# GpSimd's queue in program order, another order of seven products in the first block of a pass, and another order of tile addresses

## The chip, the cores and the metric

The kernel runs on one core of a Trainium2 chip. The core has TensorE (PE, matrix products), VectorE (DVE), ScalarE (ACT), GpSimd (POOL) and SyncE (SP); each takes its own instructions in order, and they wait for one another on semaphores. Transfers are done by 16 DMA engines; SP, ACT and POOL issue them. The metric is device time in microseconds (us). Before the change the median of three runs is 2068.01 us (2066.77 to 2068.09).

## The reference

Attention without softmax, in which keys times values are summed up along the sequence, and a mixture of experts in which all experts share one pair of weights. Cut to what matters:

```python
xn = layernorm(x)                               # 4 sequences x 1024 tokens x 1024
q = xn @ Wq.T + bq;  k = xn @ Wk.T + bk;  v = xn @ Wv.T + bv
phi_q = elu(q) + 1;  phi_k = elu(k) + 1
kv_sum = cumsum(phi_k * v, axis=1)
s = (phi_q * kv_sum) * SCALE @ Wo.T + bo
# router: top 2 of 8 experts per token, at most 256 tokens (CAP) each, in order
buf[dest] = xn[token]
h = gelu(buf @ w1.T + b1) @ w2.T + b2           # w1: 4096 x 1024, w2: 1024 x 4096
gathered = where(keep, h[dest], 0) * prob
out = zeros.at[token_idx].add(gathered)
return x + s * silu(out)
```

An expert holds at most 256 tokens, and tokens beyond that get nothing, so only the first tokens can have a g that isn't zero. The kernel works out which tokens these are, and computes queries, the result product and the feed-forward products for them alone. Everything is float32; a product of two float32 matrices is made of three products of their high and low parts (fp32r).

## The kernel before

**Two phases.** In the first (0 to 452.8 us) the keys and values of all tokens are projected (lines 160 to 162), summed up along the sequence on VectorE, transposed into tiles `kr` and stored to `kvs` in memory; the router fills lists of tokens. In the second, 140 product steps run one after another on TensorE (`multiply`, matmul in line 1005). Each step is one of the seven products of a Strassen-like scheme for a 2 x 2 block product, and has 48 matmuls of 128 x 128 by 128 x 512.

**The order of steps.** There are NP = 2 passes of 70 steps. A pass has NQ = 4 times a `hidden` block (7 steps, w1, gelu) and an `ffn_out` block (7 steps, w2), then a `queries` block (7 steps, Wq) and a `result` block (7 steps, Wo). `hidden` and `queries` go through `features`, `ffn_out` and `result` through `outputs`. The first step of pass 1 (the second pass) is n = 71, of its queries n = 127, of its result n = 134; of pass 0 they are 1, 57 and 64.

**Operands.** The left operand `a` and the right `b` of step n are two `Unit` tiles each (u = 0, 1), taken from three places in turn. `cast` (ScalarE, line 793) writes the high half, `low` (VectorE, line 796) the low half. In `features` of pass 0's first block the right operand is made in the same way, from token tiles in `work`, and then stored to memory (`xtd<-b`, line 1100, on SP) for the blocks that follow, which load it (`b<-xtd`, line 976, on SP). For pass 1 the tokens are prepared beside steps 15 to 34 by `xprep_items`: gathers on GpSimd (line 647), transposes and subtractions on VectorE, then seven split tiles `o` for each of four token blocks, stored to `xtd` on GpSimd (line 679).

**Weights.** The quarters of a weight matrix lie in five tiles `raw`. They are loaded on SP (line 766 for w1 and Wq, line 1055 for w2 and Wo), and VectorE makes the sums that the seven products need (`sub`, line 930; `plus`, line 933). `left_weights` does this for `features`: it loads the quarters (0,0), (1,0), (1,1) and (0,1) at steps n0-4 to n0-1, and makes one difference in step n0 and a sum and a difference at the start of step n0+1.

**The order by hand.** `on(n, phase, f)` hangs work onto a phase of step n, and the phases run in the order load, pre, cast0, evac, low0, add, cast1, low1, post, raw (line 905). PE, DVE, ACT and SP keep the order in which the program issues their work. GpSimd's order is left to a scheduler, except where `in_turn` (lines 233 to 236) pins an instruction, and that only outside the hand-made order. The row loads (line 1182 for `b2`, line 1272 for `bo`), the stores of line 679 and the scatters that add into `out` (line 1292) are not pinned.

**Results.** The products are summed in two PSUM tiles of four banks. `chains` says which products share one PSUM tile: in `features` the order is ROWS = (1, 6, 2, 7, 5, 4, 3) with groups (1, 2), (6, 7, 4), (5, 3). The first result of a block is copied by ScalarE to a quarter of `hid` (line 1113), the others are added by VectorE (line 933). In `result` the last quarters lie in `hid`, `ht` and `y`; they are multiplied by the gate (line 1322) and scattered to `out` by GpSimd (line 1292, four scatters a quarter). The next `hidden` block writes to the same `hid`.

**Queries.** `fetch` gathers a quarter of `kvs` into two small tiles `gk`, `turn` transposes it to two small tiles `kv` on VectorE (line 240, four instructions of 128 x 512 a quarter), ScalarE makes the exponentials (lines 1222 and 1223), and `then` joins them (lines 1228 and 1233). The quarter (0,1) is fetched at step n0+1 and turned at step n0+3.

**Small tiles.** `small` takes tiles of 4 KB a partition from a pool `sp` with nine buffers in rotation (line 896). It holds what `xprep_items` gathers, turns and splits, the temporary `t`, the rows `b2` and `bo`, `gk`, `kv`, `ex`, and the parts of the result. A new tile waits for the last user of the old one in its buffer. The pool stands ahead of `fp`, which holds three of the `raw` tiles, `y0` and the third place of a and b.

Of the kernel before, what the change touches and what calls it, by code (L numbers as in the profile page):

```python
# [18 lines left out]
P = 128  # L19
# [27 lines left out]
def tile_first_tokens(  # L47
# [43 lines left out]

    xtd = [dp.tile([7 * 2 * P, 4 * BT], F32, name=f"xtd_{p}") for p in range(NP)]

# [139 lines left out]
    def in_turn(ins):  # L233

        if not in_order[0]:
            tc.keep_in_program_order(ins)

    def turned(dst, g):

        t = nc.vector.transpose(  # L240
            dst.rearrange("p c (b j) -> p b c j", j=SQ),
            g.rearrange("p (b c i) -> p b c i", b=NA, i=SQ),
        )
        in_turn(t)

# [409 lines left out]
    def xprep_items(p, buf):  # L655

        def item(j):
            g, v = {}, {}  # L660

            def fetch():
                for i in range(2):
                    g[i] = buf(f"g{p}_{j}_{i}")
                    slots[2 * p + i].quarters(g[i], xnd, j)

            def turn():
                for i in range(2):
                    r = buf(f"x{p}_{j}_{i}")
                    turned(r.rearrange("p (c t) -> p c t", c=DC), g[i])  # L670
                    v[0, i], v[1, i] = r[:, :BT], r[:, BT:]

            def out_of(i, src):
                o = buf(f"o{p}_{j}_{i}")
                oh = o.bitcast(F32R).rearrange("p (u h k t) -> h p u k t", u=2, h=2, k=2)
                split((oh[0], oh[1]), src.rearrange("p (u k t) -> p u k t", u=2, k=2))
                dst = xtd[p].rearrange("(i u p) (s t) -> i u p s t", i=7, u=2, s=4)[i - 1]
                for u, ou in enumerate(o.rearrange("p (u s t) -> u p s t", u=2, s=4)):
                    nc.gpsimd.dma_start(dst[u, :, :, j * P : (j + 1) * P], ou)  # L679

            def plain():
                out_of(1, v[0, 0])
                out_of(2, v[1, 0])

            def sums():
                t = buf(f"t{p}_{j}")
                v["t1"], v["t2"] = t[:, :BT], t[:, BT:]
                nc.vector.tensor_tensor(v["t1"], v[0, 1], v[0, 0], ALU.subtract)
                nc.vector.tensor_tensor(v["t2"], v[1, 1], v["t1"], ALU.subtract)
                out_of(6, v["t2"])  # L690

            def sums2():
                nc.vector.tensor_tensor(v[0, 1], v[1, 1], v[0, 1], ALU.subtract)
                nc.vector.tensor_tensor(v[1, 0], v[1, 0], v["t2"], ALU.subtract)
                out_of(7, v[0, 1])
                out_of(5, v["t1"])

            def rest():
                out_of(4, v[1, 0])
                out_of(3, v[1, 1])  # L700

            return fetch, turn, plain, sums, sums2, rest

        return [item(j) for j in range(NJ)]
# [74 lines left out]
    class Unit:  # L779


        def __init__(self, side, i):

            pool = later["fu" if (i + 1) % 3 < 2 else "fp"]
            self.t = pool.tile(
                [P, 2, 2 * BT], F32R, tag=f"{side}{(i + 1) % 3}", name=name(side)
            )

# [38 lines left out]
    with tc.manual_schedule(engines=order), tc.tile_pool(name="rp", bufs=1) as rp:  # L827
# [13 lines left out]
        for b in range(nhead):  # L841
# [17 lines left out]
            if b == nhead - 1:  # L859
# [17 lines left out]
                put([[sl.load] for sl in slots], at=28 // half)  # L877
                put([[lambda i=i: left_quarter(raw[i], w1, i, 0)] for i in range(2)])
            kv_block(parts, stream, list(turn[2:]) if b == 0 else [], b == nhead - 1)
# [15 lines left out]

    sp = ctx.enter_context(tc.tile_pool(name="sp", bufs=9, reuse_waits="tile"))

    sp.tile([P, 2 * P], F32, tag="room", bufs=1, name="room")
    fp = ctx.enter_context(tc.tile_pool(name="fp", bufs=1, reuse_waits="tile"))
    later["fp"] = fp  # L900
    fps = ctx.enter_context(tc.tile_pool(name="fps", bufs=2, space=PSUM, reuse_waits="tile"))
    bq1, nbq = (cp.tile([P, DC], F32, name=n) for n in ("bq1", "nbq"))
# [13 lines left out]

    raw += [quarter(f"raw_{i}") for i in range(2, 5)]
    hid = big.tile([P, 4, NK, BT], F32, tag="xt", name="hid")
# [4 lines left out]
    yq = {(i, j): work[:, 2 * i + j] for i in range(2) for j in range(2)}  # L923
    yq[0] = quarter("y0")

# [55 lines left out]
    def tokens(p, i):  # L981
        return xtd[p].rearrange("(i u p) f -> i u p f", i=7, u=2)[i - 1]

# [31 lines left out]

    ROWS = (1, 6, 2, 7, 5, 4, 3)
    COLS = (1, 2, 6, 5, 7, 3, 4)

# [6 lines left out]

    def left_weights(n0, src, view=None):

        q = dict(zip(((0, 0), (1, 0), (1, 1), "t", (0, 1)), raw))
        raw[:] = (q[k] for k in ((0, 0), "t", (1, 0), (1, 1), (0, 1)))

        def load(*keys):
            for key in keys:
                left_quarter(q[key], src, *key)

        if n0:
            on(n0 - 4, "raw", lambda: load((0, 0)))
            on(n0 - 3, "raw", lambda: load((1, 0)))
        on(max(n0 - 2, -1), "raw", lambda: load((1, 1)))
        on(n0 - 1, "raw", lambda: load((0, 1)))

        on(n0, "add", lambda: sub(q["t"], q[0, 0], q[1, 0]))
        on(n0 + 1, "pre", lambda: plus(q[1, 0], q[1, 0], q[1, 1]))
        on(n0 + 1, "pre", lambda: sub(q[0, 0], q[1, 0], q[0, 0]))
        on(n0 + 3, "add", lambda: sub(q[0, 1], q[0, 1], q[0, 0]))
        for k, key in enumerate(((0, 0), (0, 0), (0, 1), "t", (1, 0), (1, 1), (0, 1))):
            built(n0 + 1 + k, "a", lambda key=key: q[key], by_blocks, of_blocks)

# [35 lines left out]

    def right_tokens(n0, p):
        if n0:
            for k, i in enumerate(ROWS):
                fetched(n0 + 1 + k, p, i)
            return

        x = {(i, j): work[:, 2 * j + i] for i in range(2) for j in range(2)}  # L1090
        t2 = hq["t"]
        on(1, "add", lambda: sub(x[0, 0], x[1, 1], t2))
        on(3, "add", lambda: sub(x[1, 0], x[1, 0], t2))
        keys = {1: (0, 0), 2: (1, 0), 3: (1, 1), 4: (1, 0), 5: (0, 0), 7: (0, 1)}
        for k, i in enumerate(ROWS):
            built(1 + k, "b", lambda i=i: t2 if i == 6 else x[keys[i]], by_chunks, all_chunks)

            def keep(k=k, i=i):
                for u in range(2):
                    nc.sync.dma_start(tokens(p, i)[u], flat(plan_at(1 + k)["b"][u]))  # L1100

            on(k + 1, "raw", keep)

    def features(n0, p, src, act, then=None):

        h = dict(hq)
        left_weights(n0, src)
        right_tokens(n0, p)
        chains(n0, ROWS, ((1, 2), (6, 7, 4), (5, 3)))
        ps = {k: plan_at(n0 + k)["ps"] for k in range(1, 8)}  # L1110

        def e1():
            nc.scalar.copy(whole(h[1, 0]), whole(ps[1][0]))

# [10 lines left out]
        if then:  # L1125
            for k, key, src in (
# [5 lines left out]
                )  # L1132
        on(n0 + 2, "evac", e1)
        on(n0 + 3, "evac", lambda: more(2, (0, 1), (1, 0)))
        on(n0 + 4, "evac", c11)
        on(n0 + 5, "evac", lambda: more(4, (1, 1), (1, 0)))
        on(n0 + 6, "evac", lambda: last(5, (1, 1), (1, 1)))
# [7 lines left out]
    def hidden(n0, p, s):  # L1145
# [4 lines left out]

        return features(n0, p, w1[s * DC : (s + 1) * DC], act)

# [6 lines left out]
    def ffn_out(n0, h, s, y):  # L1159
# [18 lines left out]
        if s == 0:  # L1178

            def row():  # L1180
                y["b"] = small("b2")
                nc.gpsimd.dma_start(y["b"], rows[0:1, :].broadcast_to([P, D]))

            on(n0, "load", row)
# [6 lines left out]
    def queries(n0, p):  # L1191
# [48 lines left out]
        for k, d, key in (  # L1240
            (-14, 2, (0, 0)), (-12, 2, (1, 1)), (-6, 3, (1, 0)), (1, 2, (0, 1))
        ):
# [22 lines left out]
    def result(n0, h, y, p):  # L1265
# [4 lines left out]
        def row():  # L1270
            c["b"] = small("bo")
            nc.gpsimd.dma_start(c["b"], rows[1:2, :].broadcast_to([P, D]))

# [13 lines left out]
        def done(key, parts):  # L1287
            i, j = key
            for m in range(4):
                src = parts(m)  # L1290
                apart(
                    nc.gpsimd.indirect_dma_start(  # L1292
                        out=out.rearrange("n (a f) -> (n a) f", a=2),
                        out_offset=bass.IndirectOffsetOnAxis(
                            ap=slots[2 * p + i].half[:, j, m : m + 1], axis=0
                        ),
                        in_=src,
                        in_offset=None,
                        compute_op=ALU.add,
                    ),  # L1300
# [33 lines left out]
    for p in range(NP):  # L1334
        y = dict(yq)
        if p + 1 < NP:
            prep = xprep_items(p + 1, small)
            for j, (s, at) in enumerate(
                ((s, at) for s in (1, 2) for at in ((0, 2, 2, 2, 3, 4), (2, 4, 4, 5, 5, 6)))
            ):  # L1340
                for k, (d, f) in enumerate(zip(at, prep[j])):
# [96 lines left out]
```

## Time and profile before

| what | value |
|---|---|
| median of three runs | 2068.01 us |
| profiled execution | 2073.87 us, its span 2072.1 us |
| product steps (line 1005) | 452.8 to 2049.9 us |
| TensorE busy | 1978.2 us, 95% of the span |
| VectorE busy | 1508.6 us, 73% |
| ScalarE busy | 756.9 us, 37% |
| GpSimd busy | 421.7 us, 20% |
| TensorE clock granted, mean | 0.979 |
| transfers | 360.32 MB, mean 174 GB/s |

A row of a timeline gives the start and the duration in us, the engine, the line, the operation with its output and inputs, their shapes, and the number of instructions in the row (x48). In brackets stands how long the engine had been idle before it, and what ended that. A row of windows gives, for a stretch of time, the busy time and number of instructions of each engine, then the granted TensorE clock as a share of full speed, the busy share of the 16 DMA engines, and what they moved in GB/s. The share can be a little over 1. SPq, ACTq and POOLq are the parts of those engines that issue transfers.

### The profile page before, as it was taken

How to read it: one execution, taken by the hardware profiler on the slowest of the kernel's cores; microseconds unless marked ns; L12 is line 12 of the kernel's file. 1: busy time of each engine (PE TensorE's matmuls, PEld its weight loads, DVE VectorE, ACT ScalarE, POOL GpSimd, SP SyncE). 2: the span in 40 equal slices, each digit the busy share in tenths (PEclk: the TensorE clock that was granted, in tenths of full speed). 3: DMA queues.
4: the chain of work that ended last, by engine and by line, in shares of the span. 5: the costliest groups of instructions: out<-in, count | busy, mean ns of one | idle time of the engine just before them, and what ended most of it. 6: DMA issues, size and time to landing. Idle time of an engine off the chain costs nothing.

```text
span 2072.1 us, 22267 instructions
## 1 busy us (share of the span) xinstructions
PE 1978.2 (95%) x8840; PEld 1631.3 (79%) x8840; DVE 1508.6 (73%) x1376; ACT 756.9 (37%) x874; POOL 421.7 (20%) x387
## 2 busy tenths in 40 slices
PE   7999999989999999999999889899999999999875
PEld 6877878877887887888887677788888888888764
DVE  7868876577876876975887785585685685787884
ACT  2323332225533433532423453342432432343451
POOL 1001104652003502843020068001000001120013
PEclk9999999999999999999999989999999999999988
DMA  8867849638248448447146148515515416426314
GB/s 305 242 195 234 264 124 193 190 80 347 74 147 327 156 146 328 146 163 279 54 162 256 51 103 257 209 62 197 199 61 219 167 61 248 158 82 253 133 21 63
DMA packets 114290, 360.32 MB, mean 174 GB/s; under 512 B 13216, under 2 KB 37792, under 8 KB 96032
## 3 DMA queue, kind: packets, MB, share of 16 engines
q1 hardware_dynamic: 77504, 299.98, 41.1%
q0 software_dynamic: 18240, 42.56, 7.7%
q10 hardware_dynamic: 18432, 16.26, 3.5%
q8 instruction: 72, 1.18, 0.2%
q14 instruction: 42, 0.34, 0.0%
HBM read 292.66 MB, written 73.42 MB: 177 GB/s over the span
## 4 chain that ended last, share of the span: by engine, by line
PE 79%; DVE 6%; issue 6%; POOL 3%; DMA 3%; ACT 2%; ACTq 0%; SPq 0%; DVEq 0%; POOLq 0%
PE ps L1005 61%; PE pk L160 3%; PE pk L161 3%; PE pk L162 3%; PE pv L162 3%; PE pv L160 3%; PE pv L161 3%; POOL gk L647 2%; DMA b<-xtd 2%; POOL out L1292 1%; PE pl L325 1%; DVE hid L1228 1%; DVE hid L933 1%; DVE hid L1233 1%; DMA kvs<-kr 0%
## 5 line engine op out<-in xcount | busy, mean ns | idle before, releaser
L1005 PE MATMUL ps<-b,a 128*128 128x512 f32 x6720 | 1544.5, 392 | 52.6 <-DVE y L933 19.2
L1005 PEld LDWEIGHTS ps<-b,a 128*128 128x128 f32 x6720 | 1271.3, 189 | 325.5 <-issue 26.1
L793 ACT CAST a<-raw 128x1024 fp32r<-128x1024 f32 x140 | 147.2, 1052 | 456.8 <-PE ps L1005 366.4
L647 POOL DMA_INDIRECT gk<-kvs,eighth x128 | 174.0, 1360 | 668.4 <-DVE kv L240 504.8
L796 DVE TENSOR_TENSOR a<-raw,a 128x1024 fp32r<-128x1024 f32 x140 | 170.6, 1221 | 182.7 <-ACT a L793 178.1
L793 ACT CAST a<-hid 128x1024 fp32r<-128x1024 f32 x120 | 126.1, 1051 | 368.9 <-PE ps L1005 261.1
L796 DVE TENSOR_TENSOR a<-hid,a 128x1024 fp32r<-128x1024 f32 x120 | 146.4, 1220 | 64.8 <-ACT a L793 64.6
L796 DVE TENSOR_TENSOR b<-raw,b 128x1024 fp32r<-128x1024 f32 x140 | 170.8, 1220 | 1.6 <-ACT b L793 1.6
L933 DVE TENSOR_TENSOR hid<-ps,hid 128x2048 f32<-128x2048 f32 x52 | 119.0, 2288 | 63.7 <-PE ps L1005 48.7
L930 DVE TENSOR_TENSOR raw<-raw,raw 128x2048 f32<-128x2048 f32 x70 | 160.3, 2290 | 1.1
L793 ACT CAST b<-raw 128x1024 fp32r<-128x1024 f32 x140 | 146.7, 1048 | 1.8 <-DMA xtd<-b 1.8
L933 DVE TENSOR_TENSOR work<-ps,work 128x2048 f32<-128x2048 f32 x40 | 91.5, 2288 | 48.8 <-PE ps L1005 48.8
L160 PE MATMUL pk<-xt,ws_w 128*128 128x512 f32 (+1 forms) x264 | 103.1, 391 | 2.6 <-issue 1.4
L161 PE MATMUL pk<-xt,ws_w 128*128 128x512 f32 (+1 forms) x264 | 102.9, 390 | 2.5 <-issue 1.3
L162 PE MATMUL pv<-xt,ws_w 128*128 128x512 f32 (+1 forms) x264 | 101.3, 384 | 1.3 <-DVE ws_w L167 1.2
L162 PE MATMUL pk<-xt,ws_w 128*128 128x512 f32 (+1 forms) x264 | 102.6, 388 | 0.0
L160 PE MATMUL pv<-xt,ws_w 128*128 128x512 f32 (+1 forms) x264 | 101.6, 385 | 0.0
L161 PE MATMUL pv<-xt,ws_w 128*128 128x512 f32 (+1 forms) x264 | 101.2, 383 | 0.0
L679 POOL DMA_DIRECT2D xtd<-o x56 | 41.4, 876 | 277.9 <-DVE o L167 277.2
L166 ACT CAST ws_w<-wr_w 128x1024 fp32r<-128x1024 f32 x64 | 66.1, 1048 | 82.7 <-issue 39.7
L167 DVE TENSOR_TENSOR ws_w<-wr_w,ws_w 128x1024 fp32r<-128x1024 f32 x64 | 77.8, 1215 | 14.7 <-ACT ws_w L166 11.2
L361 ACT ACTIVATE kb<-pk,bs 128x512 f32<-128x512 f32 (+1 forms) x40 | 25.8, 646 | 134.1 <-PE pk L162 97.2
(183 smaller groups left out, 1653.3 us busy)
## 6 DMA issues: line engine op xcount, KB each, us to landing
b<-xtd SPq DMA_DIRECT2D x126, 1024.0 KB
raw<-in_w SPq DMA_DIRECT2D x64, 1024.0 KB
wr_w<-in_wk SPq DMA_DIRECT2D x32, 512.0 KB
wr_w<-in_wv SPq DMA_DIRECT2D x32, 512.0 KB
xtd<-b SPq DMA_DIRECT2D x14, 1024.0 KB
xtd<-o POOLq DMA_DIRECT2D x56, 256.0 KB
kvs<-kr ACTq DMA_DIRECT2D x32, 256.0 KB
raw<-in_wq SPq DMA_DIRECT2D x8, 1024.0 KB
```

The source lines that it names most:

```text
L160: nc.tensor.matmul(ps, ws[:, 0, k], mv[:, 0, k, c0:c1], start=k == 0, stop=False)
L161: nc.tensor.matmul(ps, ws[:, 0, k], mv[:, 1, k, c0:c1], start=False, stop=False)
L162: nc.tensor.matmul(ps, ws[:, 1, k], mv[:, 0, k, c0:c1], start=False, stop=k == DC - 1)
L166: nc.scalar.copy(dst[0], src)
L167: nc.vector.tensor_tensor(dst[1], src, dst[0].bitcast(F32), ALU.subtract)
L647: nc.gpsimd.indirect_dma_start(out=dst, out_offset=None, in_=src, in_offset=bass.IndirectOffsetOnAxis(ap=idx, axis=0),)
L679: nc.gpsimd.dma_start(dst[u, :, :, j * P : (j + 1) * P], ou)
L793: nc.scalar.copy(self.parts[0], src)
L796: nc.vector.tensor_tensor(self.parts[1], self.src, self.parts[0].bitcast(F32), ALU.subtract)
L930: nc.vector.tensor_tensor(dst, a, b, ALU.subtract)
L933: nc.vector.tensor_tensor(dst, a, b, ALU.add)
L1005: nc.tensor.matmul(ps[:, m], a(h, k, m), b(l, k), start=s["first"] and u == 0 and k == 0 and i == 0, stop=u == 1 and k == 1 and i == 2, sk ...
```

## The change

**GpSimd's queue.** `in_turn` now always keeps an instruction in the program's order, and the stores of line 679, the row loads and the scatters to `out` go through it as well. In the old order of instructions, 32 gathers of `gk` for pass 1 stand between `out<-c` and the scatters of `hid`, `ht` and `y`; in the new one these twelve scatters come directly after `out<-c`, then the load of `b2`, then the gathers.

**One store a tile.** The rows of `xtd` are laid out so that both units of a product lie in one row. Each `o` is stored by one transfer and not by two (28 in place of 56). The loads of b stay as large as they were.

**Preparation in smaller items.** `xprep_items` returns nine functions for a token block and not six, and they are hung on steps as `ats` says.

**The first hidden block of a pass.** It takes its products in the order FIRST, with chains (1), (2), (6, 5, 3), (7, 4). Its weights are loaded in the order (0,0), (0,1), (1,0), (1,1), and the sums are made later: one difference in the add phase of step n0+1, one in its post phase, the sum in step n0+2. Its results come in another order, with one more addition on VectorE.

**Addresses.** `fp` is made first, with the tiles `room`, `row` and the third places of a and b (`a2`, `b2`) at its start, then `y0` and three `raw` tiles in another order; `sp` comes behind it, with eight buffers. `b2`, `bo` and `t` share the tile `row`. By the addresses of the two programs, `a2` and `b2` lay on the last `kr` tiles before, and lie on buffers of the first phase's weights and tokens after.

**Queries.** The quarter (0,1) is turned at step n0+4 and not n0+3.

```diff
-    xtd = [dp.tile([7 * 2 * P, 4 * BT], F32, name=f"xtd_{p}") for p in range(NP)]
+    xtd = [dp.tile([7 * P, 2 * 4 * BT], F32, name=f"xtd_{p}") for p in range(NP)]
...
     def in_turn(ins):
-        if not in_order[0]:
-            tc.keep_in_program_order(ins)
+        tc.keep_in_program_order(ins)
+        return ins
...
-                dst = xtd[p].rearrange("(i u p) (s t) -> i u p s t", i=7, u=2, s=4)[i - 1]
-                for u, ou in enumerate(o.rearrange("p (u s t) -> u p s t", u=2, s=4)):
-                    nc.gpsimd.dma_start(dst[u, :, :, j * P : (j + 1) * P], ou)
+                dst = xtd[p].rearrange("(i p) (s t) -> i p s t", i=7, s=8)[i - 1]
+                in_turn(
+                    nc.gpsimd.dma_start(
+                        dst[:, :, j * P : (j + 1) * P], o.rearrange("p (s t) -> p s t", s=8)
+                    )
+                )
...
-                t = buf(f"t{p}_{j}")
+                t = one(f"t{p}_{j}")
...
-            pool = later["fu" if (i + 1) % 3 < 2 else "fp"]
-            self.t = pool.tile(
-                [P, 2, 2 * BT], F32R, tag=f"{side}{(i + 1) % 3}", name=name(side)
-            )
+            place = (i + 1) % 3
+            tag = f"{side}{place}"
+            self.t = later.pop(tag, None)
+            if self.t is None:
+                pool = later["fu" if place < 2 else "fp"]
+                self.t = pool.tile([P, 2, 2 * BT], F32R, tag=tag, name=name(side))
...
-                put([[lambda i=i: left_quarter(raw[i], w1, i, 0)] for i in range(2)])
+                put([[lambda i=i: left_quarter(raw[i], w1, 0, i)] for i in range(2)])
...
-    sp = ctx.enter_context(tc.tile_pool(name="sp", bufs=9, reuse_waits="tile"))
-    sp.tile([P, 2 * P], F32, tag="room", bufs=1, name="room")
     fp = ctx.enter_context(tc.tile_pool(name="fp", bufs=1, reuse_waits="tile"))
     later["fp"] = fp
+    fp.tile([P, 2 * P], F32, name="room")
+    later["row"] = fp.tile([P, D], F32, tag="row", name="row")
+    later.update(
+        (f"{side}2", fp.tile([P, 2, 2 * BT], F32R, tag=f"{side}2", name=f"{side}2"))
+        for side in "ab"
+    )
...
-    raw += [quarter(f"raw_{i}") for i in range(2, 5)]
+    y0 = quarter("y0")
+    last_raw = quarter("raw_4")
+    raw += [quarter("raw_2"), last_raw, quarter("raw_3")]
+    sp = ctx.enter_context(tc.tile_pool(name="sp", bufs=8, reuse_waits="tile"))
...
+    def one(n):
+        t = later.pop("row", None)
+        return fp.tile([P, D], F32, tag="row", name=name(n)) if t is None else t
...
+    FIRST = (1, 2, 6, 7, 5, 4, 3)
...
+        if order == ROWS:
+            tiles = ((0, 0), (1, 0), (1, 1), "t", (0, 1))
+            loads = ((-4, (0, 0)), (-3, (1, 0)), (-2, (1, 1)), (-1, (0, 1)))
+            on(n0, "add", lambda: sub(q["t"], q[0, 0], q[1, 0]))
+            on(n0 + 1, "pre", lambda: plus(q[1, 0], q[1, 0], q[1, 1]))
+            on(n0 + 1, "pre", lambda: sub(q[0, 0], q[1, 0], q[0, 0]))
+        else:
+            tiles = ((0, 0), (0, 1), (1, 0), (1, 1), "t")
+            loads = ((-4, (0, 0)), (-3, (0, 1)), (-2, (1, 0)), (-1, (1, 1)))
+            on(n0 + 1, "add", lambda: sub(q["t"], q[0, 0], q[1, 0]))
+            on(n0 + 1, "post", lambda: sub(q[0, 0], q[1, 1], q["t"]))
+            on(n0 + 2, "add", lambda: plus(q[1, 0], q[1, 0], q[1, 1]))
+        on(n0 + 3, "add", lambda: sub(q[0, 1], q[0, 1], q[0, 0]))
...
-        on(1, "add", lambda: sub(x[0, 0], x[1, 1], t2))
-        on(3, "add", lambda: sub(x[1, 0], x[1, 0], t2))
+        on(3, "add", lambda: sub(x[0, 0], x[1, 1], t2))
+        on(4, "add", lambda: sub(x[1, 0], x[1, 0], t2))
...
+            chains(n0, order, ((1,), (2,), (6, 5, 3), (7, 4)))
...
+            on(n0 + 2, "evac", lambda: e1((0, 1)))
+            on(n0 + 3, "evac", lambda: last(2, (0, 0), (0, 1)))
+            on(n0 + 4, "evac", lambda: more(3, (1, 0), (0, 1)))
+            on(n0 + 5, "evac", lambda: more(4, (1, 1), (0, 1)))
...
-                y["b"] = small("b2")
-                nc.gpsimd.dma_start(y["b"], rows[0:1, :].broadcast_to([P, D]))
+                y["b"] = one("b2")
+                in_turn(nc.gpsimd.dma_start(y["b"], rows[0:1, :].broadcast_to([P, D])))
...
-            (-14, 2, (0, 0)), (-12, 2, (1, 1)), (-6, 3, (1, 0)), (1, 2, (0, 1))
+            (-14, 2, (0, 0)), (-12, 2, (1, 1)), (-6, 3, (1, 0)), (1, 3, (0, 1))
...
-                ((s, at) for s in (1, 2) for at in ((0, 2, 2, 2, 3, 4), (2, 4, 4, 5, 5, 6)))
+            ats = ((0, 2, 2, 2, 2, 3, 3, 3, 4), (2, 4, 4, 5, 4, 5, 5, 6, 6))
```

## The prediction

> **What bounds the kernel now.** I read the page's span and group lists first, then TensorE's timeline from 452 us on, then the timelines of the engines named as releasers. The profiled span is 2072.1 us, its device time 2073.87 us, the median of the runs 2068.01 us; I add up against the span and take the difference off the median.
>
> ```profile
> span 2072.1 us, 22267 instructions
> L1005 PE MATMUL ps<-b,a 128*128 128x512 f32 x6720 | 1544.5, 392 | 52.6 <-DVE y L933 19.2
> ```
>
> Line 1005 holds all 140 product steps, 48 matmuls each. It runs from 452.8 to 2049.9 us, 1597.1 us. The timeline shows what a step costs unhindered and where it is hindered:
>
> ```profile
> 468.05 0.73 PE L1005 MATMUL ps<-b,a 128*128 128x512 f32 x1 [4.22 <-ACT b L793]
> ...
> 659.38 11.14 PE L1005 MATMUL ps<-b,a 128*128 128x512 f32 x48 [1.88 <-DMA b<-xtd]
> 671.33 141.70 PE L1005 MATMUL ps<-b,a 128*128 128x512 f32 x624 [0.81 <-DMA b<-xtd]
> 815.53 317.43 PE L1005 MATMUL ps<-b,a 128*128 128x512 f32 x1392 [2.49 <-DMA b<-xtd]
> ...
> 1195.63 0.76 PE L1005 MATMUL ps<-b,a 128*128 128x512 f32 x1 [9.42 <-DVE y L933]
> ...
> 1306.13 622.83 PE L1005 MATMUL ps<-b,a 128*128 128x512 f32 x2736 [6.50 <-DMA b<-xtd]
> ```
>
> 141.70/624 is 0.227 us a matmul, so 10.88 us a step and 1523 us for 140: TensorE is the bound, and about 74 us are lost at named places. Before 477.9 us 73 matmuls take 25.1 us where 16.5 would do: **8.6 us at the start**. At the pass boundary 99 matmuls from 1286.9 to 1320.4 take 33.5 us against 22.4: **11 us**. Steps 19, 20 and 33, beside the preparation of pass 1's tokens, lose about 7. The two ends of a pass (1168 to 1198 and 1963 to 1994) lose 21 and 22. The change can gain only in these places; anything it adds elsewhere must outlast its cover.
>
> **The start: two waits removed, -8.6, residue 0.5 (0 to 4).**
>
> ```profile
> 466.01 1.04 ACT L793 CAST a<-raw 128x1024 fp32r<-128x1024 f32 x1 [16.29 <-DMA kvs<-kr]
> ```
>
> The second step's first cast waits 16.29 us for stores of `kr`. In the old addresses tiles a2 and b2, which that cast writes, lie on the last `kr` tiles; in the new ones they come right behind `row`, on buffers of the first phase that TensorE last reads at 452.8. A second cause is that the three VectorE passes at 456.8 to 463.7 (3 x 2.29) stood ahead of the low halves; `FIRST` needs quarter (0,0) for steps 1 and 3 and (0,1) for step 2, so no difference is due until step 3. The quarter that SyncE loaded at 465.44 loses the same neighbour. In the new order ScalarE issues the stores 455.1 to 458.5, casts a and b (2 x 1.05) until 460.6, VectorE's lows (2 x 1.22) until 463.0 at the latest, and step 2 begins at 452.8 + 11.0 = 463.8. Step 3 wants q00 = q11 - t, then its low half: 469.2 + 2 x 1.2 and a cast, about 472.8, before 474.7; 2 us of cover. If that is gone, or if the stores `xtd<-b` still hold ScalarE's b cast (6.59 us at 475.54), up to 4 us stay. I take 0.5: **-8.1**.
>
> **The pass boundary: -11, residue 2.5 (0 to 6).**
>
> ```profile
> 1271.17 1.62 POOL L1292 DMA_INDIRECT out<-hid,half  x1 [0.30 <-issue]
> 1285.43 2.29 DVE L933 TENSOR_TENSOR hid<-ps,hid 128x2048 f32<-128x2048 f32 x1 [12.52 <-DMA out<-hid,half]
> 1291.14 1.46 SPq L1055 DMA_DIRECT2D raw<-in_w  x2
> ```
>
> `hid` is finished on VectorE at 1237.1, but its scatter is issued at 1271.17, because the 32 gathers of `gk` for a far later step come first in GpSimd's queue (1211 to 1271, each 0.94 to 3 us). VectorE therefore waits 12.52 us to overwrite `hid`; the subtractions behind it are late, so is SyncE's weight load at 1291.14 (it follows VectorE's 1288.77 pass), and the token loads queued behind that load; TensorE then waits 6.50. Kept in program order, `out<-hid`, `ht`, `y` (12 scatters, about 1.6 us each) stand right behind `out<-c`, at about 1237 to 1270, and the gathers after them. The scatter lands some 20 us before `hid` is wanted, so the chain above goes.
>
> What is late next is the DMA. Four scatters keep the engines full for some 8 us (0.95 share in 2036 to 2044). Three sets are 24 us; the window 1237 to 1270 already carries 20.8 us of 33, of which the departing gathers are 3 to 4. So 24 + 17 is 41 in 33: about 8 us spill past 1270, while each token load has one step, 10.9 us, of lead. That fits, narrowly. A wait of 2 us is likelier than none, since steps 19 and 33 waited 1.88 and 2.49 at shares near 1.0; after the 2.49 the clock stood at 0.84 and cost 1.8 more. I take 2.5: **-8.5**.
>
> The Trainium skill ("DMA: Bandwidth & Descriptors", Queues, rings and completion order, Arbitration) says that each DMA engine takes turns between its queues a packet at a time. By it scatters take up to half the service from the token loads that they now run beside, which speaks against the new order; no run here shows the split. Its sum: a load of 5.3 us per step at half rate needs 10.6 of the 10.9, so no wait and 2.5 less than I take, with nothing to spare.
>
> **The ends of a pass: +2.64 each, +5.3 (0 to 7).** With eight instead of nine small tiles the last `kv` transposes move from step n0+3's place to n0+4's.
>
> ```profile
> 1108.02 2.64 DVE L240 STREAM_TRANSPOSE kv<-gk 128x512 f32<-128x512 f32 x4
> ...
> 1117.91 2.73 DVE L1228 SCALAR_TENSOR_TENSOR hid<-ps,bq,hid 128x512 f32<-128x512 f32 x4 [4.36 <-ACT hid L1222]
> ```
>
> At 1108 they cost nothing: VectorE idles 1.66 and 4.36 us behind them. Their new place is after the low half at 1125.15 and before the `hid<-ps` of 1126.28. From 1117.9 to 1138.8 VectorE has no gap; ScalarE's exponentials then start 3.68 us late on `hid` (1137.72), the next cast follows them, and the chain runs VectorE, ScalarE, VectorE until the 9.42 us wait at 1195.63. Four transposes are 2.64 us in that chain. It is 0 if VectorE turns out to have slack there, 3.5 if the longer stall keeps the clock down longer (0.50 to 0.63 there now). I take 2.64, since the rows are contiguous.
>
> **Steps 15 to 34: 0 (-3 to +3).** GpSimd issues 28 stores of a whole tile in place of 56 (0.7 us an issue; GpSimd is 20% busy, off the path). Bytes stay the same. The items are spread over more phases, which moves gathers off the stretch at share 1.0, but eight tiles make `o` copies and one token tile wait for an older store. ScalarE waits there already 6.7 us on a store (660.98 and 816.50) while TensorE loses 1.9 to 2.5. Casts finish about 4 us before their step; that is the cover. From the same rows: all of 3 us gained, or one more such wait.
>
> **Hidden at no cost.** One more 2.29 us addition per first block: VectorE is busy about 3 of 11 us in steps 72 and 73, and in steps 3 and 4 fills gaps of 3.4 and 3.8; uncovered it would be 2 x 2.29. The single `row` tile: b2's load waits for bo's last reader (1195), and the load has until step 79. `out` scatters at the very end had no gathers before them, so the 22 us tail (2049.9 to 2072.1) stays.
>
> **The sum.** -8.1 - 8.5 + 5.3 + 0 = -11.3: span 2060.8, and 2068.0 - 11.3 = **2056.7 us**. Best ends together: -8.6 - 11 + 0 - 3 = -22.6, 2045.4. Worst: -4.6 - 5 + 7 + 3 = +0.4, 2068.4.
>
> **The rivals.**
>
> *The boundary gives its gain back (0.15).* The same scatters now meet the token loads and the gathers meet steps 73 to 77, where weight loads start. For it: share 1.05 to 1.12 from 1275 to 1300 already. Against: GB/s there is 223 to 317, so bytes are not the limit, and the total demand is unchanged. If 8.5 falls to 2: 2063.
>
> *The transposes are absorbed (0.15).* The b loads' own wait (2.19 at 1135.14) could be what sets step 62, and the exponentials hide the rest. Against: VectorE's gapless 21 us. Time 2056.7 - 5.3 = 2051.4.
>
> *Eight tiles and a strict GpSimd queue block the preparation (0.09), slower.* Place: steps 17 to 20 and 31 to 34. A copy to `o` on ScalarE waits for the landing of an older store (6.7 us as at 660.98), the casts and VectorE's lows queue behind it, GpSimd cannot pass the next store with gathers, and TensorE stops. Price: 6.7 in each of four items if the 4 us of cover is already used by the waits of before: 26.8 - 11.3 = +15.5, 2083. It makes the kernel slower than before from 2.8 us per item on, measurably from 3.9. For it: a wait of this length exists, with nine tiles. Against: spreading the items gives each store longer to land.
>
> *The change doesn't do what it says (0.06).* Another tile on the `kr` memory, or another wait behind ScalarE's first cast, keeps the start, and a scatter held in order behind a later wait keeps the boundary: only +5.3 and the preparation would be left, less a few us, near 2068.
>
> **How the numbers follow.** The forecast has 0.55. 0.2% is 4.1 us, about what a measurement of this kernel can tell from no change: faster means under 2063.9. The forecast, absorbed transposes and most of the boundary rival lie there, less their upper edges: 0.82. Same (to 2072.1): the rest of these and most of the last rival, 0.09. Slower: 0.09. The range reaches from 2049, since both best ends together are unlikely, to 2066, which holds the boundary rival and leaves out the blocked preparation; the forecast's own range is 2052 to 2061.
>
> **What would show it.** In the new profile: no ScalarE cast waits on `kvs<-kr` after 455, and TensorE has no wait over 1 us before 480. `out<-hid` is issued near 1237 less the shift, VectorE's wait on it is gone, the token wait of step 75 is under 3 us. Four transposes stand in VectorE's gapless run near 1117 to 1129, the wait for `y` is unchanged or longer, and the pass ends lose 23 to 25 us each. ScalarE's waits on `xtd<-o` stay below 8 us. I am wrong if any of these readings turns, and most if TensorE shows waits on `a` or `b` from ScalarE in steps 17 to 34.

## The result, and the profile after

| | before | after |
|---|---|---|
| median | 2068.05 us (2066.77 to 2068.89) | 2051.79 us (2049.46 to 2053.1) |
| profiled execution, its span | 2073.87, 2072.1 us | 2053.1, 2051.3 us |
| product steps | 452.8 to 2049.9 us | 444.7 to 2029.9 us |

The changed kernel takes 0.9921 of the time before (95% interval 0.9903 to 0.9938), 16.3 us less. The forecast was 11.3 less, 2056.7, in a range from 2049 to 2066. From the page of the changed kernel, and from TensorE's timeline (start, duration, line, tiles, number of matmuls, and in brackets the wait ahead):

```profile
span 2051.3 us, 22262 instructions
L1023 PE MATMUL ps<-b,a 128*128 128x512 f32 x6720 | 1541.1, 392 | 44.2 <-DVE y L951 20.7
```

```profile
643.36 154.22 PE L1023 MATMUL ps<-b,a 128*128 128x512 f32 x672 [2.08 <-DMA b<-xtd]
800.11 317.43 PE L1023 MATMUL ps<-b,a 128*128 128x512 f32 x1392 [2.54 <-DMA b<-xtd]
...
1182.59 0.76 PE L1023 MATMUL ps<-b,a 128*128 128x512 f32 x1 [10.48 <-DVE y L951]
1184.77 720.72 PE L1023 MATMUL ps<-b,a 128*128 128x512 f32 x3167 [1.41 <-DVE b L802]
```

The row of 3167 matmuls from 1184.77 on runs across the pass boundary without a wait; before, three rows with waits of 0.94, 0.38 and 6.50 us stood there. A step begins with the first of its 48 matmuls, and 10.88 us is the median step of each of these profiles. The time between the starts of two steps, less 10.88 us a step, is what the stretch between them loses. A wait ahead of a step counts for the step before it. The second and third profile of the kernel before are from experiments 1 and 10:

| us lost in steps | before, three profiles | after | forecast |
|---|---|---|---|
| 1 to 18 (start) | 10.8, 11.5, 10.9 | 2.9 | -8.1 |
| 19 to 32 (preparation) | 3.8, 6.8, 4.0 | 4.4 | 0 |
| 33 to 61 | 4.1, 5.1, 3.7 | 2.9 | 0 |
| 62 to 66 (end of pass 0) | 21.0, 21.2, 21.9 | 25.2 | +2.6 |
| 67 to 77 (boundary) | 11.0, 11.5, 9.8 | 0.0 | -8.5 |
| 78 to 131 | 1.1, 1.2, 1.2 | 1.3 | 0 |
| 132 to 140 (end of pass 1) | 21.9, 21.8, 22.9 | 25.2 | +2.6 |
| tail after the last matmul | 22.3, 21.9, 22.6 | 21.5 | 0 |

Against the mean of the three, the steps gain 13.8 us and the tail 0.8. The rest up to 16.3 is not the change's: the first phase ended at 452.8, 445.2 and 442.7 us in three profiles of one kernel, and at 444.7 after. In the first of them VectorE and ScalarE stood still from 416 to 422 and TensorE almost; that execution was 5.9 us longer than the median.

### The profile page after: what moved, and what is told of

It reads as the page before. It is cut to its first block, busy times and chain, and to the rows that moved or that the text cites. A ratio compares the mean times of both kernels' runs of the same rounds, so it can differ in the third digit from the quotient of the medians.

```text
span 2051.3 us, 22262 instructions
## 1 busy us (share of the span) xinstructions
PE 1968.8 (96%) x8840; PEld 1624.9 (79%) x8840; DVE 1513.0 (74%) x1378; ACT 756.7 (37%) x874; POOL 398.3 (19%) x359
## 4 chain that ended last, share of the span: by engine, by line
PE 78%; DVE 11%; ACT 3%; DMA 3%; issue 3%; POOL 0%; ACTq 0%; SPq 0%; DVEq 0%; POOLq 0%
PE ps L1023 62%; PE pk L160 3%; PE pk L161 3%; PE pk L162 3%; PE pv L162 2%; PE pv L160 2%; PE pv L161 2%; DMA b<-xtd 1%; DVE hid L951 1%; DVE a L802 1%; DVE hid L1263 1%; DVE b L802 1%; DVE raw L948 1%; DMA xtd<-b 1%; PE pl L326 1%
## 5 line engine op out<-in xcount | busy, mean ns | idle before, releaser
L1023 PEld LDWEIGHTS ps<-b,a 128*128 128x128 f32 x6720 | 1269.0, 189 | 315.9 <-ACT b L799 21.5
L648 POOL DMA_INDIRECT gk<-kvs,eighth x128 | 156.4, 1222 | 657.8 <-DVE kv L240 620.0
L951 DVE TENSOR_TENSOR hid<-ps,hid 128x2048 f32<-128x2048 f32 x54 | 123.5, 2286 | 54.4 <-PE ps L1023 54.4
L680 POOL DMA_DIRECT2D xtd<-o x28 | 24.2, 888 | 283.3 <-DVE o L167 276.3
```

The source lines that it names most:

```text
L648: nc.gpsimd.indirect_dma_start(out=dst, out_offset=None, in_=src, in_offset=bass.IndirectOffsetOnAxis(ap=idx, axis=0),)
L951: nc.vector.tensor_tensor(dst, a, b, ALU.add)
L1023: nc.tensor.matmul(ps[:, m], a(h, k, m), b(l, k), start=s["first"] and u == 0 and k == 0 and i == 0, stop=u == 1 and k == 1 and i == 2, sk ...
```

## The experiments

Times are medians. The kernel before ran in the same rounds each time, and took 2066.56 us beside experiments 1 to 4, 2083.22 beside 5 and 6, 2080.84 beside 7 to 9, and 2067.84 beside 10 to 12; those of 5 to 9 ran on one and the same other chip. Times are compared within a group, or by their ratio to the kernel before.

### 1. The kernel before, again

> The kernel before, profiled a second time. In its first profile the product steps begin at 452.8 us, in the changed kernel's at 444.7, and TensorE, VectorE and ScalarE all stand still near 416 to 422 us. Theory: that stop belongs to the one execution (its 2073.87 us are 5.9 over the median), so here the steps begin at 445 to 448 and the span is 2065 to 2068. Rival: the change shortens the first phase by 8 us; then the steps begin near 452.8 again.

2068.02 us, ratio 1.0003 (0.9993 to 1.0012); the steps begin at 445.2. The 8 us by which the first phase seemed shorter after the change belong to one execution. The expected span of 2065 to 2068 was missed (2069.3), in part because step 33 waited 4.97 us for its tokens here and 2.49 in the first profile.

### 2. GpSimd's queue free again

```diff
     def in_turn(ins):
-        tc.keep_in_program_order(ins)
+        if not in_order[0]:
+            tc.keep_in_program_order(ins)
         return ins
```

> The changed kernel with GpSimd's order left to the scheduler again (stores, row loads and scatters not pinned); all else stays. Theory: the boundary's gain of about 10.4 us comes from the scatters' place, so 10 us or more come back, 2062 to 2072, and it can be over 10.4, because the new product order copies a result into hid one step earlier, on ScalarE, which then waits for the scatter of hid. Rival: the gain comes from the other order of products or of addresses; then the time stays within 2 us of 2051.8.

2063.07 us, ratio 0.9985 (0.9976 to 0.9995), by ratio 13 us over the changed kernel; steps 67 to 77 lose 13.0 us in place of 0.0. The timelines of GpSimd, ScalarE and TensorE:

```profile
1252.53 3.75 POOL L1329 DMA_INDIRECT out<-hid,half  x1 [0.30 <-issue]
...
1269.32 1.86 ACT L1141 COPY hid<-ps 128x2048 f32<-128x2048 f32 x1 [18.00 <-DMA out<-hid,half]
...
1271.23 644.28 PE L1024 MATMUL ps<-b,a 128*128 128x512 f32 x2832 [10.65 <-ACT hid L1141]
```

The scatter of `hid` is issued behind the gathers; ScalarE, which FIRST lets write `hid` one step earlier than VectorE did, waits 18.00 us for it, and TensorE 10.65. So the boundary's gain is the queue's, and FIRST needs the queue.

### 3. The old order of products, at the new addresses

```diff
-            n0, p, w1[s * DC : (s + 1) * DC], act, order=ROWS if s else FIRST
+            n0, p, w1[s * DC : (s + 1) * DC], act, order=ROWS
```

The first two quarters are loaded as (0,0), (1,0), and the token differences are made in steps 1 and 3, as before.

> The changed kernel with the old order of seven products (ROWS) in the first block of both passes; the new addresses and queue stay. Theory: both causes act at the start; three VectorE passes of 2.29 us stand ahead of the low halves again, the low half of step 2's b ends some 2.5 us after step 1 does, TensorE waits 2 to 4 us in all and its clock falls: +3 to +6, 2055 to 2058. Rival: the addresses alone did it; then TensorE waits under 1 us and the time is within 1 us of 2051.8. At the boundary no change by either.

2057.75 us, ratio 0.9947 (0.993 to 0.9964), by ratio 5.4 us more than the changed kernel; steps 1 to 18 lose 8.0 and not 2.9, the boundary still 0.0.

```profile
453.61 2.29 DVE L948 TENSOR_TENSOR raw<-raw,raw 128x2048 f32<-128x2048 f32 x1
...
455.99 1.04 ACT L799 CAST a<-raw 128x1024 fp32r<-128x1024 f32 x1 [13.92 <-DVE raw L948]
...
458.03 0.49 PE L1023 MATMUL ps<-b,a 128*128 128x512 f32 x1 [1.89 <-ACT b L799]
```

ScalarE's first cast no longer waits for the stores of `kr`, but for VectorE's third weight sum, because in ROWS step 2 reads the result of that sum (q00). VectorE's place in the queue, as I had put it, is only half of it: the sum is an input of step 2.

### 4. The old order of pools, with the new order of products

```diff
+    sp = ctx.enter_context(tc.tile_pool(name="sp", bufs=8, reuse_waits="tile"))
+    sp.tile([P, 2 * P], F32, tag="room", bufs=1, name="room")
     fp = ctx.enter_context(tc.tile_pool(name="fp", bufs=1, reuse_waits="tile"))
...
-    later.update(
-        (f"{side}2", fp.tile([P, 2, 2 * BT], F32R, tag=f"{side}2", name=f"{side}2"))
-        for side in "ab"
-    )
...
+    raw += [quarter(f"raw_{i}") for i in range(2, 5)]
     y0 = quarter("y0")
-    last_raw = quarter("raw_4")
-    raw += [quarter("raw_2"), last_raw, quarter("raw_3")]
```

> The changed kernel with the pools in the old order (small tiles first, then the weight tiles, a2 and b2 last), eight small tiles and the shared row tile kept. Theory: step 2's cast waits some 16 us for the stores kvs<-kr again, TensorE waits 4 us or more at step 2 and its clock falls: +5 to +9, 2057 to 2061. Rival: the order of products alone did it; then TensorE waits under 1 us at step 2 and the time is within 1 us of 2051.8.

2068.94 us, ratio 1.0008 (0.9997 to 1.0018): 18 us more than the changed kernel, twice what was expected, and no better than the kernel before, though the boundary keeps its gain (0.1 us lost). Steps 1 to 18 lose 19.5. SyncE, ScalarE, VectorE and TensorE:

```profile
449.30 31.94 SPq L1119 DMA_DIRECT2D xtd<-b  x5
...
464.00 1.04 ACT L799 CAST a<-raw 128x1024 fp32r<-128x1024 f32 x1 [20.70 <-DMA kvs<-kr]
...
465.08 1.23 DVE L802 TENSOR_TENSOR a<-raw,a 128x1024 fp32r<-128x1024 f32 x1 [14.77 <-ACT a L799]
...
466.05 0.80 PE L1018 MATMUL ps<-b,a 128*128 128x512 f32 x1 [8.63 <-ACT b L799]
...
470.59 2.29 DVE L943 TENSOR_TENSOR raw<-raw,raw 128x2048 f32<-128x2048 f32 x1 [3.15 <-DMA kvs<-kr]
...
477.44 1.05 ACT L799 CAST a<-raw 128x1024 fp32r<-128x1024 f32 x1 [9.55 <-DVE raw L943]
```

The cast waits 20.70 us for `kvs<-kr`. In the kernel before, VectorE used that wait for its three weight sums; under FIRST they stand behind the low halves, so VectorE idles 14.77 us, starts the sums at 470.59 after 3.15 us more on a store of `kr`, and step 3's cast waits another 9.55 for them. The stores themselves are late too: by the list of transfers those that ScalarE issues from 448.70 on take up to 20.1 us to land, against at most 8.5 in experiment 1. Beside them run the stores `xtd<-b`, which SyncE issues from 449.30 on here and only from 458.59 on in experiment 1, behind a weight load. In experiment 3 they begin at 449.70, and a store of `kr` takes 19.5. That the one delays the other was not tested by itself. The four corners of steps 1 to 18:

| us lost | ROWS | FIRST |
|---|---|---|
| old addresses | 10.8 to 11.5 | 19.5 |
| new addresses | 8.0 | 2.9 |

FIRST alone costs about 8 us, the addresses alone gain 3, both together gain 8. The parts cannot be priced one by one. The corners are not quite pure: the upper left one is the kernel before, with nine small tiles, its own GpSimd order and no `row`, and the other three have eight, the new order and `row`.

### 5 and 8. The transposes back at step n0+3

```diff
-                t.append(small("kv"))
+                t.append(one("kv") if (i, j) == (0, 1) and half == 0 else small("kv"))
...
-            (-14, 2, (0, 0)), (-12, 2, (1, 1)), (-6, 3, (1, 0)), (1, 3, (0, 1))
+            (-14, 2, (0, 0)), (-12, 2, (1, 1)), (-6, 3, (1, 0)), (1, 2, (0, 1))
```

One of the two tiles lies in `row`, which is idle there, so nine places are at hand.

> The changed kernel, with the last transposes of kv back at step n0+3, where they were; the first of the two tiles that they write is the row tile, which nothing else holds between b2's last use and bo's load. Theory: the transposes cost 2.64 us in each pass end where they stand now, so this is 4.5 to 6 us faster than the changed kernel, 2046 to 2047.5; TensorE loses about 20 us at each pass end again, as before the change. Rival: bo's load now waits for the last use of kv and comes too late for the first result, which gives it back; then VectorE waits for bo in front of the first rows of the result and the time is 2050 or more.

2080.08 us beside 2083.22 of the kernel before, far from 2046: TensorE, VectorE and ScalarE stopped together in the first phase (the steps begin at 461.5) and in steps 74 to 77 (15.7 us lost). The part under test moved as expected: steps 62 to 64 lose 3.9 (6.4 after the change), 132 to 134 3.9 (6.2). The same kernel beside the changed one:

> The kernel of e5_turn_back again, beside the changed kernel on the same chip. Theory: 4 to 6 us faster than the changed kernel in the same rounds, from the two pass ends (e5's trace lost 3.9 us in steps 62 to 64 and in 132 to 134, against 6.4 and 6.2 in the changed kernel). Rival: the gain is taken back by bo's later load, within 1 us of the changed kernel.

2073.91 us (ratio to before 0.9968, 0.995 to 0.9986) against 2078.32 of the changed kernel in the same rounds: 4.4 us. The intervals of the two ratios overlap (0.9968 to 1.0009 for the changed kernel), so it is the traces that show the gain: steps 62 to 64 and 132 to 134 lose 3.9 and 4.0 here, 6.3 and 6.2 in the changed kernel beside it.

### 6 and 9. The queue alone, on the kernel before

```diff
     def in_turn(ins):
-        if not in_order[0]:
-            tc.keep_in_program_order(ins)
+        tc.keep_in_program_order(ins)
+        return ins
...
-                    nc.gpsimd.dma_start(dst[u, :, :, j * P : (j + 1) * P], ou)
+                    in_turn(nc.gpsimd.dma_start(dst[u, :, :, j * P : (j + 1) * P], ou))
```

This is made in the kernel before; the row loads and scatters are pinned in the same way, and nothing else is changed.

> The kernel before, with one thing changed: GpSimd's stores, row loads and scatters in the program's order. Theory: the boundary's loss of 10.5 us goes to under 1 and nothing else moves, so 9 to 11 us faster than before, 2056 to 2058. Rival: without the other changes the queue blocks elsewhere, the row load in front of the stores of kr at the start or the stores of the preparation, and less than 7 us are gained.

> The kernel of e6_queue_alone again, beside the changed kernel on the same chip. Theory: 9 to 11 us faster than the kernel before, all of it between steps 67 and 77 (10.5 us lost before, under 1 here). Rival: with the gathers moved behind the scatters a stop of all engines takes the gain back, as in e6, where 8 of 10 us stayed lost in steps 74 to 77.

2079.17 and 2077.58 us, ratios 0.9987 (0.9977 to 0.9997) and 0.9985 (0.9969 to 1.0002): about 3 us gained and not 10. In steps 67 to 77 9.5 and 9.0 us stay lost, with a stop near 1320 in place of the wait for tokens. On that chip the rival of experiment 9 holds. Up to the stop the trace does show the queue's effect. TensorE and VectorE in experiment 6:

```profile
1206.89 109.97 PE L1006 MATMUL ps<-b,a 128*128 128x512 f32 x474 [1.41 <-DVE b L797]
...
1285.39 2.29 DVE L934 TENSOR_TENSOR hid<-ps,hid 128x2048 f32<-128x2048 f32 x1 [3.13 <-PE ps L1006]
```

VectorE overwrites `hid` without waiting for its scatter (12.52 us before), and TensorE runs 474 matmuls without a wait; in the kernel before, the first wait came after 383 and the 6.50 us for tokens after 431. So the queue alone removes both waits. What that is worth in time where no stop follows was not measured; experiment 2, which takes the queue away, prices it.

### 7. The changed kernel beside them

> The changed kernel again, beside the two that follow. When these two were first measured the kernel before took 2083 us, 16 more than in the other measurements, and in both traces TensorE, VectorE and ScalarE stood still together for 8 to 15 us, once near 400 to 420 and once near 1302 to 1327, both times while GpSimd issued a long row of gathers. Theory: these stops belong to that chip or hour and hit each kernel with gathers; where they are absent this takes 2049 to 2053 beside 2065 to 2069 before. Rival: the change moves the gathers of gk into a stretch where they stop the other engines; then this shows a stop behind 1257 too.

2078.32 us, ratio 0.9989 (0.9968 to 1.0009): on that chip the change gains next to nothing. Its steps 67 to 77 lose 14.4 us and not 0.0, and its first phase is 10.7 us longer. GpSimd, TensorE, ScalarE and VectorE, and the windows (busy time of PE, PEld, DVE, ACT and POOL, each with its instructions, then the clock, the share of the DMA engines in use, and GB/s):

```profile
1302.91 0.95 POOL L648 DMA_INDIRECT gk<-kvs,eighth  x1 [0.30 <-issue]
1304.17 0.95 POOL L648 DMA_INDIRECT gk<-kvs,eighth  x1 [0.30 <-issue]
...
1304.30 0.58 PE L1023 MATMUL ps<-b,a 128*128 128x512 f32 x1 [0.81 <-issue]
1305.70 0.59 PE L1023 MATMUL ps<-b,a 128*128 128x512 f32 x1 [0.81 <-issue]
...
1312.08 1.99 ACT L799 CAST a<-raw 128x1024 fp32r<-128x1024 f32 x2 [16.55 <-remote]
...
1312.08 2.29 DVE L951 TENSOR_TENSOR hid<-ps,hid 128x2048 f32<-128x2048 f32 x1 [15.29 <-remote]
```

```profile
1300.00:1310.00 10.00, 4.24 (x9) 2.38 (x9) 0.00 (x0) 0.00 (x0) 6.73 (x8) 0.57 0.37 129
```

TensorE issues one matmul in 1.4 us and waits for nothing that the profile shows; VectorE and ScalarE do nothing for 15 us; GpSimd goes on gathering until 1308, and the transfers are at 0.37. It is not the wait for tokens that the prediction's rival named: the transfers have room. Nor does a load of instructions end the stop: the list of transfers, which names them as a kind of their own, has none between 1291 and 1332. The stop lies behind 1257, as the rival of this experiment said.

### 10 to 12. The kernel before, late gathers, and the transposes back

```diff
             g = kvt["g", i, j] = [small("gk") for _ in range(2)]
+            if p:
+                for t in g:
+                    nc.vector.memset(t[:, :1], 0.0)
```

This edit of experiment 11 stands on top of that of 5; 12 is the kernel of 5.

> The kernel before, profiled beside the two that follow. Where the kernel before takes 2080 us or more, it has never been profiled. Theory: there its gathers of gk (1211 to 1271) run beside the result block and stop nothing, so only the stop of the first phase, 10 to 13 us, is added to 2066, and the change's boundary stop of 12 to 19 us is its own. Rival: the kernel before has a second stop in steps 66 to 73 there, and the gain lost is noise of the place. Where the kernel before takes 2066, no stop over 6 us is expected.

> The kernel of e5_turn_back, and the gathers of gk for pass 1 held back to the steps where the program puts them (112 to 117, some 400 us later) by a tiny VectorE write to each gk tile. Theory: the stop of all engines in steps 74 to 77 needs the gathers beside the scatters, the token loads and the weight loads of the boundary (transfers busy at 1.0 and more), so without the gathers there it is gone: where the kernel before takes 2080 or more, 12 to 19 us faster than e12 in the same rounds; elsewhere within 2 us of e12. Rival: a long row of gathers stops the engines wherever it stands; then the stop moves to steps 112 to 117. Second rival: the gathers have no part in it and the stop stays in steps 74 to 77.

> The kernel of e5_turn_back a third time, for the same rounds as e11. Where the kernel before takes 2066: 2046 to 2048. Where it takes 2080 or more: 2074 to 2080, with 14 to 19 us lost in steps 74 to 77.

2067.1, 2046.67 and 2046.38 us. This chip showed no stop, so experiments 10 and 11 do not tell what causes it: the gathers of 11 ran from 1682 to 1798 as meant, at no difference to 12. Experiment 12 has the ratio 0.9898 (0.9882 to 0.9914), the changed kernel 0.9921; with experiment 11 it is the fastest of the study, faster than both kernels. VectorE and GpSimd in it:

```profile
1093.05 2.64 DVE L240 STREAM_TRANSPOSE kv<-gk 128x512 f32<-128x512 f32 x4
1097.35 1.23 DVE L802 TENSOR_TENSOR a<-raw,a 128x1024 fp32r<-128x1024 f32 x1 [1.66 <-ACT a L799]
1102.94 2.73 DVE L1263 SCALAR_TENSOR_TENSOR hid<-ps,bq,hid 128x512 f32<-128x512 f32 x4 [4.36 <-ACT hid L1257]
...
1168.24 0.58 POOL L1307 DMA_DIRECT2D bo<-in_rows  x1 [112.76 <-DVE hid L1268]
...
1175.97 2.35 DVE L951 TENSOR_TENSOR e<-ps,bo 128x1024 f32<-128x1024 f32 x2
```

The idle 1.66 and 4.36 us stand behind the transposes again. The load of `bo` now waits for VectorE's last use of `kv`, but its first reader comes 7.7 us later and doesn't wait.

## Why the prediction was right, step by step

**The start, -8.1: measured -8.2** (11.0 on average to 2.9). Steps 1 to 3 alone lose 8.7, 9.0 and 8.9 before and 0.0 after, so the residue of 0.5 is not there; most of the 2.9 is the token wait ahead of step 19 (2.08). The wait of step 2's first cast on `kvs<-kr` is gone. ScalarE issues the stores of `kr` until 451.2 and casts at once, and TensorE runs through:

```profile
444.66 98.11 PE L1023 MATMUL ps<-b,a 128*128 128x512 f32 x432
...
447.22 3.96 ACTq L425 DMA_DIRECT2D kvs<-kr  x4
451.22 1.05 ACT L799 CAST a<-raw 128x1024 fp32r<-128x1024 f32 x1 [9.41 <-PE ps L1023]
```

The two causes were named, but treated as two waits that each add something; experiments 3 and 4 show that the addresses alone gain 3 us and FIRST alone costs 8.

**The boundary, -8.5: measured -10.8** (10.8 on average to 0.0). The mechanism held: `out<-hid` is issued 0.8 us after VectorE has finished it (1222.36 + 2.29), and the gathers come last. Mis-sized was the residue of 2.5 us, a token wait from busy transfers; there was none. VectorE, GpSimd and ScalarE of the changed kernel, then windows:

```profile
1222.36 2.29 DVE L1359 TENSOR_TENSOR hid<-hid,work 128x2048 f32<-128x2048 f32 x1
...
1225.40 1.81 POOL L1328 DMA_INDIRECT out<-hid,half  x1 [27.53 <-issue]
...
1254.15 1.87 ACT L1140 COPY hid<-ps 128x2048 f32<-128x2048 f32 x1
...
1257.85 1.02 POOL L648 DMA_INDIRECT gk<-kvs,eighth  x1 [0.30 <-issue]
```

```profile
1235.00:1245.00 10.00, 10.00 (x46) 8.26 (x45) 6.07 (x5) 2.11 (x2) 7.08 (x4) 1.00 1.06 257
...
1275.00:1285.00 10.00, 10.00 (x46) 8.28 (x45) 4.08 (x3) 1.59 (x2) 7.87 (x8) 1.00 1.03 399
```

The spill was there, and longer than the 8 us that I had reckoned: the share stays at 0.90 to 1.09 from 1235 to 1295. Yet by the list of transfers the median token load lands in 8.3 us beside the scatters (1225 to 1262) and in 7.8 us beside the gathers (1270 to 1295), within its lead of 10.9. The Trainium skill ("DMA: Bandwidth & Descriptors", Queues, rings and completion order, Arbitration) has the queues take turns. The sum by it, no wait, is what came out, though the loads were faster than the 10.6 us of that sum; how the queues shared the engines no run shows.

**The ends of a pass, +5.3: measured +6.8** (+3.8 for steps 62 to 66, +3.0 for 132 to 140), and 4.4 to 4.8 us come back when the transposes go back (8 against 7, 12 against the changed kernel by ratio, from other rounds). In the traces of 12 and the changed kernel it is 2.5 us in steps 62 to 64 and 2.2 in 132 to 134, close to the 2.64 each of the forecast. Another 1.1 us of steps 62 to 64 (2.8 before, 3.9 in experiment 12) stays when the transposes are back, and its cause is open. The four transposes stand where the working had them, with no idle time on either side:

```profile
1109.73 1.22 DVE L802 TENSOR_TENSOR a<-raw,a 128x1024 fp32r<-128x1024 f32 x1
1110.87 2.49 DVE L240 STREAM_TRANSPOSE kv<-gk 128x512 f32<-128x512 f32 x4
1113.27 2.25 DVE L951 TENSOR_TENSOR hid<-ps,hid 128x2048 f32<-128x2048 f32 x1
```

So the rival that they are absorbed falls.

**The preparation, 0: no change that stands out.** Steps 15 to 34 lose 7.6, 12.0 and 7.4 before and 8.4 after; the 12.0 holds the wait of 4.97 us of experiment 1. By the table, steps 19 to 61 gain 1.9 on the mean of the three and 0.5 on the first profile and the third. Eight tiles and one store a tile did not block it: step 33 waits 2.54 us against 2.49, and ScalarE's longest wait on a store of `o` is 7.0 us against 6.7. The slower rival falls.

**The rest.** The sum of the parts is -13.8 in the steps against -11.3: the boundary gives 2.3 more, the stretch beside and behind the preparation 1.9 more, and the ends of a pass take 1.5 more. So the sum came out closer than its parts, which is luck. The tail's 0.8 has no explanation here, and 1.7 up to the median lie within the interval of the ratio (-13 to -20 us). The median of 2051.79 lies in the range, and 0.2 under the narrower 2052 to 2061 that the forecast gave for itself. One step of its working does not come out: 141.70/624 is 10.90 us a step. The 10.88 that it used is right all the same, as the median step.

## What to carry to other kernels

A long-lived buffer's first wait is set by what lay at its address before: look at which release its first writer waits for, and put it over something that is done early. Where an engine's order is left to a scheduler, look for cheap early work, such as gathers for a far later step, that stands ahead of a store whose buffer is wanted soon. An edit that fills a wait and one that removes the wait should be measured together, since each alone can be worth little, or less than nothing.

## What was not expected of the hardware

On one chip the kernel before took 2081 to 2083 us and not 2066 to 2068. In each of experiments 5 to 9, all on that chip, VectorE and ScalarE stood still together for 6 to 20 us at a time, and TensorE almost, while GpSimd issued a long row of gathers: once in the first phase, between 389 and 416, and once between 1290 and 1327. The second stop ended within 4 us of the end of the last gather each time. Gathers alone are not enough, since 32 of them run beside steps 35 to 40 (835 to 890 us) in experiment 7 and steps 33 to 61 lose 3.1 us there, as elsewhere. Nor are full transfers alone: in the middle of the stop of experiment 7 the share is 0.37. It was 1.00 in 1280 to 1290, shortly ahead of it, but the changed kernel ran through such a stretch (1.03 in 1275 to 1285) elsewhere without a stop. What the engines wait for is not in the profile.

Whether the kernel before has only the first of the two stops there was not seen, as it was not profiled on that chip. An estimate points to it: the kernel takes 13 to 17 us longer there, and in the traces of 5 to 9 the first phase ends at 455.4 to 461.5 and not at 442.7 to 446.4 (experiments 1 to 4 and 10 to 12), 9 to 19 us later, so that little is left for a second stop. If that is so, the second stop comes with the gathers' new place behind the scatters, as the rival of experiment 7 has it. It stays open, and with it how much of the boundary's gain is safe: 10.8 us in one place, while in the other the stop of 9.0 to 19.5 us stands where it was won.
